# Moving the start of the second layer into the last steps of the first layer's end, and reordering the row sums of the opening stage

## The chip, the cores and the metric

The kernel runs on one core of one Trainium2 chip. The metric is device time in microseconds (us). Before the change three runs took 2792.45, 2796.39 and 2797.21 us; the median is 2796.39. One further execution was recorded by the hardware profiler, and every duration below comes from that record. The engines are called PE (TensorE, matrix products), DVE (VectorE), ACT (ScalarE), POOL (GpSimd) and SP (SyncE, which here only issues transfers). Each engine takes its instructions in the order in which they are queued.

## What is computed

Two graph attention layers on 4096 nodes with 512 features, in fp32. Cut to what matters:

```python
# layer 0
h = relu(layernorm(x))
node_att = softmax(h @ node_w, axis=0)
e = (h @ edge_w) @ (h @ edge_w).T          # 4096 x 4096
e = where(adj > 0, e, -9e15)
x = x + adj * (node_att * softmax(e, axis=1)) @ (h @ weight) + bias
# layer 1, 8 heads of 64
h = relu(layernorm(x))
data1 = (h @ W.T + b).reshape(N, 8, 64)
src, trg = sum(data1 * src_proj, -1), sum(data1 * trg_proj, -1)     # N x 8
e = src.T[:, :, None] + trg.T[:, None, :]
e = where(e >= 0, e, 0.01 * e) + adj                                 # adj as a bias
x = x + concat over heads of softmax(e, axis=-1) @ data1
```

In layer 1 the score is a sum of a source and a target logit but for the leaky step, so its exponential is the larger of two products of a factor of the source node and a factor of the target node. The kernel works with these, with the target logits shifted by their maximum over all nodes (for each head). It calls the target's factors column factors (g, d and what is derived from them) and the source's row factors (z and u).

## The kernel before the change

The 4096 rows are 32 tiles of 128. A block is 512 rows, so there are 8 blocks of 4 tiles. The work goes through five stages, and inside each the instructions stand in an order written by hand.

**Stage 0** (to about 230 us; `fetch`, `stats`, `norm`, `send`, `pull`, `turn`, `row_sums`, `product`, `parts_of`, `step`). Each tile is normalised and transposed, and h is multiplied by `weight` and `edge_w`. From block 1 on, the two products are done by a scheme with seven half-size products per weight instead of eight. It needs four sums of sub-blocks of h for each block (`row_sums`, L251 to L254, on DVE) and sums of the weights (`weight_sums`; its last part, L226, on DVE, overwrites a quarter of the weights once block 0, which uses the plain product, is done). PE's order in block 1 is: products 1 and 2, which need no sums; product 6, which needs the second row sum; product 5, which needs the first row sum and L226; then 7, 3, 4. `step(t)` queues on each engine what tile t and the tiles ahead of it need. `step(6)` turns tiles 6 and 7, and `step(7)` does block 1's row sums before more statistics. `turn` for the first eight tiles ends with `logit` (L158, DVE; L161, POOL), the node attention's logit and the bias sum. The tiles h lie in a ring of four buffers, x in a ring of six.

**Scores of layer 0** (about 230 to 640 us, L538) and **its weighted sums** (to about 1470 us, L751) are not touched by the change.

**The linear stage of layer 1** (`tail`, `linear`, `values`, `logits`, `turn_h`; about 1470 to 1586 us). One step per tile s: DVE adds the bias to the tile before (L894) and turns the next h (L880, a transpose of 32 x 32 squares); PE multiplies tile s by w1 (L887, 8 instructions); POOL multiplies the finished values by the target and the source projection (L898, two products); DVE reduces each per head two steps later (L903), into t_m and s_n. Four PSUM banks hold the results in turn. The output, layernorm and h of layer 0's last block are finished beside the first 20 steps (`ending`). At its end the target maximum is found: a reduction over t_m (L972), a transpose on PE (L978), a reduction, a spread over the partitions by PE (L983) and a copy.

**Layer 1** (L1097 to L1395). For each of 4 blocks of 1024 output nodes and each of 2 sets of 4 heads there is one group of 32 steps, eight groups in all. One step (i, m) takes one tile m of 128 target nodes: `load` (SP, four steps ahead), `exps` (ACT, exp of the adjacency bias into PSUM, L1119), `factors` (ACT, L1129 for head 3 and L1155 for head 0), `weigh` (DVE, up to four products in the order head 3, 0, 1, 2; L1189, and L1186 for head 0; in every fourth step head 0 is done by ACT and POOL), `scale` (POOL for the first steps, then ACT: two heads' values times d), `sums` and the sum of head 3 (POOL), and `gather` (PE, 32 instructions L1223 in two halves and 8 of L1228). `weigh` runs one step ahead of `gather`, `factors` two. Head 3's product reads two SBUF tensors (z and e); the others read z or rl from SBUF and ex from PSUM. Each kind of product has two buffers (head 0: three). At a group's end PE's sums are copied out by ACT: the first quarter in `gather` (L1260), the other three and the denominators one step later in `copy_rest` (L1270, L1272). `tables` prepares the row factors of the later groups in the first steps of group 0.

Between the linear stage and the first step stand the shift by the maximum, the column factors (L1398 to L1406, 128 x 256 elements), the row factors of four heads (L1394, L1395, L1408, L1409) and the first step's four products.

## Time and profile before

| what | value |
|---|---|
| median of three runs | 2796.39 us |
| the profiled execution | 2791.45 us, of it 2789.7 from its first to its last instruction (the span) |
| one step of the linear stage, start to start | 3.43 us |
| end of the last linear product | 1586.03 us after the start |
| end of the second step's products on DVE | 1605.46 us |
| one group of layer 1, from the third on | 146.5 us |

How to read the views. In the list of groups and in the order of time, a row has the start, the duration, the engine, the line of the kernel, the operation and its tiles, then how often; square brackets hold the idle time ahead of it and what ended that. In the list of waits a row has the engine and its line, what it waited for, and the total, the count and the longest in us. In tables by window each engine has its busy time and its count of instructions, followed by the share of full clock that PE was granted, the share of the DMA queues and their rate.

### The profile page before, as it was taken

To read this page: it belongs to the slowest core of one execution; us is meant where nothing else is said; L and a number is where in the kernel's file an instruction comes from. 1 tells how busy PE (TensorE), PEld (TensorE's weight loads), DVE (VectorE), ACT (ScalarE), POOL (GpSimd) and SP (SyncE) were. 2 spreads that over 40 slices of the span, in tenths; PEclk is the share of its full clock that TensorE was granted. 3 is DMA by queue.
4 is the path that set the end of the run, shared out by engine and by line. 5 is a ranking of instruction groups with operands and counts; after the bars stand their busy time and mean duration, and the time that the engine had idled before them with its cause. 6 is when DMAs were issued, how large, how long until landed. Compare 5 with 4: busy or idle time off the path is not lost. (4 is left out here: it accounts for less than half of the span.)

```text
span 2789.7 us, 48939 instructions
## 1 busy us (share of the span) xinstructions
PE 2747.3 (98%) x17835; PEld 1758.8 (63%) x17835; DVE 2504.7 (90%) x3425; ACT 1475.5 (53%) x2218; POOL 1465.5 (53%) x1250
## 2 busy tenths in 40 slices
PE   7999999999999999999999899999999999999999
PEld 4885444445888888888885323464646464655555
DVE  7877789899988888888886799999999999999998
ACT  2212233333133333433332288998888888888786
POOL 5322344444010010111107698888989897979796
PEclk9999999999999999999999899999999999999999
DMA  5636898888999999999967279999999998989897
GB/s 175 177 106 245 292 321 308 303 304 268 206 215 195 201 262 190 234 257 214 236 191 196 81 192 241 241 230 240 222 241 230 242 233 236 229 243 227 217 221 172
DMA packets 536001, 630.00 MB, mean 226 GB/s; under 512 B 292152, under 2 KB 346456, under 8 KB 535760
## 3 DMA queue, kind: packets, MB, share of 16 engines
q1 hardware_dynamic: 461920, 415.87, 49.9%
q0 software_dynamic: 71824, 207.07, 34.4%
q10 hardware_dynamic: 2016, 3.93, 0.4%
q8 instruction: 140, 2.29, 0.3%
q14 instruction: 101, 0.83, 0.1%
HBM read 404.23 MB, written 107.15 MB: 183 GB/s over the span
## 5 line engine op out<-in xcount | busy, mean ns | idle before, releaser
L1223 PE MATMUL pv<-pr,sup 128*32 128x512 f32 x8192 | 1074.1, 594 | 9.7 <-DVE ngd_m L1178 5.5
L1223 PEld LDWEIGHTS pv<-pr,sup 128*32 128x32 f32 x8192 | 503.3, 110 | 411.0 <-issue 163.4
L1189 DVE SCALAR_TENSOR_TENSOR pr<-z,g_m,ex 128x1024 f32<-128x1024 f32 x512 | 630.4, 1270 | 1.5 <-PE dn L1228 0.7
L1200 POOL TENSOR_TENSOR acc<-acc,pr 128x1024 f32<-128x1024 f32 x240 | 576.3, 2401 | 95.0 <-DVE pr L1189 90.5
L1228 PE MATMUL dn<-pr,d_m 128*2 128x512 f32 x1984 | 411.8, 592 | 0.0
L538 PE MATMUL pe<-he_t,he_t 128*128 128x512 f32 x896 | 386.2, 592 | 0.0
L712 ACT ACTIVATE d<-d 128x1024 f32<-128x1024 f32 x126 | 133.1, 1056 | 424.4 <-DVE d L704 222.8
L1189 DVE SCALAR_TENSOR_TENSOR pr<-z,g_m,e 128x1024 f32<-128x1024 f32 x256 | 348.4, 1361 | 0.4 <-ACT e L1129 0.4
L1119 ACT ACTIVATE ex<-e 128x1024 f32<-128x1024 f32 x256 | 263.2, 1028 | 152.7 <-DVE pr L1189 151.7
L538 PEld LDWEIGHTS pe<-he_t,he_t 128*128 128x128 f32 x896 | 169.3, 190 | 210.3 <-issue 194.0
L1129 ACT ACTIVATE e<-e,ld_m 128x1024 f32<-128x1024 f32 x256 | 291.1, 1137 | 0.0
L751 PE MATMUL po<-sup,u 128*128 128x256 f32 x1024 | 263.3, 379 | 0.0
L751 PE MATMUL po<-he_t,at 128*128 128x256 f32 x1024 | 262.9, 379 | 0.0
L1186 DVE SCALAR_TENSOR_TENSOR pr<-rl,ngd_m,ex 128x1024 f32<-128x1024 f32 x191 | 242.7, 1270 | 3.0 <-ACT ex L1119 2.5
L751 PE MATMUL po<-sup,at 128*128 128x256 f32 x1024 | 242.3, 379 | 2.6 <-DVE mc L544 1.5
L840 POOL DMA_DIRECT2D he_t<-he_t x56 | 48.8, 949 | 355.3 <-ACT he_t L754 303.6
L1155 ACT ACTIVATE rl<-z,ngd_m,d_m 128x1024 f32<-128x1024 f32 x191 | 234.9, 1230 | 0.0
L722 DVE TENSOR_TENSOR at<-d,a 128x1024 f32<-128x1024 f32 x126 | 154.2, 1224 | 74.9 <-PE po L751 40.8
L751 PEld LDWEIGHTS po<-sup,at 128*128 128x128 f32 x1024 | 194.2, 190 | 30.0 <-DVE at L722 2.2
L751 PEld LDWEIGHTS po<-he_t,at 128*128 128x128 f32 x1024 | 194.4, 190 | 26.8 <-issue 0.3
L751 PEld LDWEIGHTS po<-sup,u 128*128 128x128 f32 x1024 | 193.9, 190 | 26.1
L543 POOL DMA_DIRECT2D er_d<-mk x136 | 75.0, 551 | 228.9 <-DVE rm L540 216.9
(275 smaller groups left out, 4006.6 us busy)
## 6 DMA issues: line engine op xcount, KB each, us to landing
e<-in_adj_t_dram SPq DMA_DIRECT2D x256, 512.0 KB, 6.2
acc<-pr POOLq DMA_DIRECT2D x192, 512.0 KB, 6.7
a<-in_adj_t_dram SPq DMA_DIRECT2D x126, 512.0 KB, 5.3
ac<-in_adj_t_dram SPq DMA_DIRECT2D x124, 256.0 KB, 4.9
ar<-in_adj_dram SPq DMA_DIRECT2D x120, 256.0 KB, 4.6
ec_d<-mc POOLq DMA_DIRECT2D x120, 256.0 KB, 4.9
er_d<-mk POOLq DMA_DIRECT2D x112, 256.0 KB, 4.5
et<-er_d SPq DMA_DIRECT2D x448, 64.0 KB, 4.1
```

Of the source, the lines that this page charges most:

```text
L538: nc.tensor.matmul(pe[:, :w], he_t[i][:, k, (t % TB) * P:(t % TB + 1) * P], he_t[j][:, k, BL - w:], start=(k == 0), stop=(k == KC - 1))
L712: nc.scalar.activation(d, d, AF.Exp)
L722: nc.vector.tensor_tensor(w, d, aj.pop((n, q)), ALU.mult)
L751: nc.tensor.matmul(acc[:, j, :], A[:, j * P:(j + 1) * P], B, start=(first_ and j == 0), stop=last, skip_group_check=True)
L1119: nc.scalar.activation(x_, ra.pop((i, m)), AF.Exp)
L1129: nc.scalar.activation(x_, ra[i, m], AF.Exp, bias=ld_m[:, h // HG, m:m + 1])
L1155: nc.scalar.activation(r, zs_[i, 0], AF.Relu, bias=ngd_m[:, h // HG, m:m + 1], scale=d_m[:, h, m:m + 1])
L1186: nc.vector.scalar_tensor_tensor(w, rl.pop((i, m)), ngd_m[:, h // HG, m:m + 1], x_, op0=ALU.subtract, op1=ALU.mult)
L1189: p_ = nc.vector.scalar_tensor_tensor(w, zs_[i, k], g_m[:, h + k, m:m + 1], e3.pop((i, m)) if k == 3 else x_, op0=ALU.max, op1=ALU.mult)
L1200: nc.gpsimd.tensor_tensor(acc[i, 3], acc[i, 3], w, ALU.add)
L1223: nc.tensor.matmul(v[c][q][col * Q:(col + 1) * Q, :], va[:, m, g * HG + k, c0:c0 + Q], pr[i, m, k][:, q * BL:(q + 1) * BL], start=(m == 0) ...
L1228: nc.tensor.matmul(dn[col * Q:col * Q + w.shape[1], :], w, src, **fl)
```

## The change

In stage 0, `step(6)` does block 1's row sums and the source weights' last sum right behind the two tiles it turns; the logits of tiles 6 and 7 are held for `step(7)`, with the edge weights' sum. In the linear stage, the weights w1 and the target projection are folded to 512 x 8 weights, and the last eight tiles' target logits are computed from h itself, early, by small products on PE; the maximum, the column factors of the first 24 tiles, the row factors and the first step's products of layer 1 are then made in steps 23 to 31. The last eight columns' factors are made inside layer 1, behind the products of its third step. Two PSUM banks instead of four hold the linear results. Layer 1's buffers lie over those of layer 0. In six steps ACT makes the source reduction instead of DVE. At a group's end two quarters instead of one are copied out at once.

```diff
@@ stage 0
-            logit(t, h)
+            if t < T0 - 2:
+                logit(t, h)
+            else:
+                held.append((t, h))
...
                 if t == T0 - 2:
                     turn(t)
                     turn(t + 1)
-                elif t != T0 - 1:
+                    row_sums(t // TB)
+                    weight_sums("s", ws, last=True)
+                elif t == T0 - 1:
+                    weight_sums("e", we, last=True)
+                    for t_h in held:
+                        logit(*t_h)
+                else:
                     turn(t)
-                if t % TB == TB - 1:
-                    row_sums(t // TB)
+                    if t % TB == TB - 1:
+                        row_sums(t // TB)
...
-        weight_sums("s", ws, last=True)
-        weight_sums("e", we, last=True)
@@ layer 1's buffers (he_t: layer 0's; he_t[2] holds b, the two projections and tab)
+        "pr0": [at_(he_t[3], 1), at_(he_t[2], 0)],
+        "pr2": [at_(he_t[1], 1), at_(he_t[2], 1)],
+        "e3": [flat(ats[0]), at_(he_t[0], 0)],
...
@@ the linear stage
-            vps[t] = bank(PR[t % TB])
+            vps[t] = bank(PR[2 + t % 2])
...
-                eng = nc.vector if t == NT - 1 and key == "t" else nc.gpsimd
-                eng.tensor_tensor(prs[t, key], v, wt[key], ALU.mult)
+                nc.gpsimd.tensor_tensor(prs[t, key], v, wt[key], ALU.mult)
...
+                if key == "s" and t in BY_ACT:
+                    for h in range(H):
+                        nc.scalar.activation(heads(a)[:, h, :], heads(a)[:, h, :], AF.Copy, accum_out=dst[:, h, t:t + 1])
...
+        BY_ACT = range(14, 26, 2)
+        T1 = NT - 2 * TB
+        def prepare(s):
+            if 1 <= s <= KC:
+                nc.gpsimd.tensor_tensor(he_t[4][:, s - 1, :], wt["w1"][:, s - 1, :], wt["t"], ALU.mult)
+            if s == KC + 1:
+                nc.gpsimd.tensor_tensor(he_t[5][:, 0, :], wt["b"], wt["t"], ALU.mult)
+            if KC < s <= 2 * KC:
+                nc.vector.tensor_reduce(wp[:, s - KC - 1, 0:H], heads(he_t[4][:, s - KC - 1, :]), AX.X, ALU.add)
...
+        def early_tiles(s):
+            for k in range(2 * TB):
+                if s == (9 + k if k < TB else 14 + k):
+                    nc.sync.dma_start(he_t[1][:, k % TB, :], h_d[T1 + k])
+                if s == (14 + k if k < TB else 17 + k):
+                    nc.vector.transpose(he_t[3][:, k % TB, :].rearrange("p (k a q) -> p k a q", k=KC, q=S),
...
+        def early_logits(s):
+            for n in range(2):
+                if s == (18, 24)[n]:
...
+                    for k in range(KC):
+                        for g in range(TB):
+                            nc.tensor.matmul(banks["e"][g * S:(g + 1) * S, n * P:(n + 1) * P], wp[:, k, :],
+                                             he_t[3][:, g, k * P:(k + 1) * P], start=(k == 0), stop=(k == KC - 1))
...
+        def column_rest(lo, hi):
+            nc.scalar.activation(d_m[:, :, lo:hi], t_m[:, :, lo:hi], AF.Exp, scale=SLOPE)
+            nc.vector.tensor_scalar(nlg_m[:, :, lo:hi], t_m[:, 0::HG, lo:hi], -(1.0 - SLOPE), None, ALU.mult)
+            nc.vector.scalar_tensor_tensor(ngd_m[:, :, lo:hi], g_m[:, 0::HG, lo:hi], -1.0, d_m[:, 0::HG, lo:hi],
...
+        def layer_1(s):
...
+            if s == 25:
+                nc.vector.tensor_reduce(em, banks["e"][:, 0:2 * P], AX.X, ALU.max)
+                nc.vector.tensor_scalar(x4, gsel, em, None, ALU.mult)
+                nc.vector.tensor_reduce(tm1, t_m[:, :, 0:T1], AX.X, ALU.max)
+                nc.vector.tensor_tensor(tm1, tm1, tb, ALU.subtract)
+                banks["t"] = bank(7)
+                nc.tensor.transpose(banks["t"][:H, 0:P], tm1, ident)
+                nc.tensor.matmul(banks["t"][:H, P:P + TB], sel[:, 0:H], x4, start=True, stop=True)
+                nc.scalar.activation(q_row, ra[0, 0], AF.Exp)
+            if s == 26:
+                nc.vector.tensor_reduce(tmx, banks["t"][:H, 0:P + TB], AX.X, ALU.max)
+                banks["b"] = bank(3)
+                nc.tensor.matmul(banks["b"][:, 0:H], tmx.to_broadcast([H, P]), ident[:H, :H], start=True, stop=True)
+            if s == 27:
+                nc.vector.tensor_tensor(tmb, banks["b"][:, 0:H], tb, ALU.add)
+                column_factors(0, T1)
+                row_factor(3)
+                column_exps(0, T1)
...
+            if s == 28:
+                column_rest(0, T1)
...
+            if s >= 29:
+                first_weigh((3, 0, 1)[s - 29])
+                if s < 31:
+                    first_values(s - 29)
...
-        logits(NT - 2, "t")
-        nc.vector.tensor_reduce(tm1, t_m[:, :, 0:NT - 1], AX.X, ALU.max)
+        logits(NT - 2)
+        first_weigh(2)
         values(NT - 1)
-        logits(NT - 1, "t")
...
@@ layer 1
+                if (i, m, k) == (0, 1, 2):
+                    logits(NT - 1)
...
-                nc.scalar.copy(os_[0][0], v[0][0])
+                for q in range(HV):
+                    nc.scalar.copy(os_[0][q], v[0][q])
...
+                if s == 1 and f is weigh:
+                    column_factors(T1, NT)
+                    column_exps(T1, NT)
+                    column_rest(T1, NT)
```

## The prediction, made before the changed kernel was run

> **What bounds the kernel now.** I read the busy time of the engines first, then the chain that ended last, then TensorE's (PE's) list of waits, then the order of time around each wait.

> ```profile
> PE 2747.3 (98%) x17835; PEld 1758.8 (63%) x17835; DVE 2504.7 (90%) x3425; ACT 1475.5 (53%) x2218; POOL 1465.5 (53%) x1250
> ...
> PE pv L1223 28%; PE dn L1228 8%; DVE pr L1189 3%; PE pt L1299 1%; ACT e L1129 1%; DVE pr L1186 0%; DMA acc<-pr 0%; ACT rl L1155 0%; DVE pr L1367 0%; POOL lg L1144 0%; POOL acc L1200 0%; PE pv L1299 0%; PE pt L1281 0%; ACT ex L1119 0%; ACT z L1395 0%
> ```

> PE is busy 98% of the span, so only its idle time and its slow time can be won, unless another engine sets a stage's pace. The waits are few:

> ```profile
> PE pv L1223 <- DVE ngd_m L1178: 5.5, 1, 5.5
> PE bank L267 <- DVE he_t L252: 3.5, 1, 3.5
> PE pv L1223 <- ACT rl L1155: 3.1, 1, 3.1
> PE po L978 <- DVE tm L976: 2.9, 1, 2.9
> ...
> PE bank L267 <- DVE ws L226: 2.1, 1, 2.1
> ```

> They lie in two places: stage 0 (L267) and the passage to layer 1 (the others). The same two places run on half a clock. Columns below: window, its length, the busy times, then PE's clock, DMA share, GB/s.

> ```profile
> 56.00:62.00 6.00, 3.85 (x9) 2.62 (x9) 5.33 (x11) 1.54 (x3) 1.81 (x2) 0.50 0.75 224
> ...
> 1588.20:1588.50 0.30, 0.00 (x0) 0.00 (x0) 0.00 (x1) 0.00 (x0) 0.30 (x1) 0.65 0.00 0
> 1588.50:1605.00 16.50, 7.10 (x27) 1.93 (x31) 15.10 (x26) 13.10 (x14) 6.87 (x11) 0.50 0.25 78
> ...
> 1600.00:1746.00 146.00, 143.10 (x1262) 46.09 (x1266) 146.00 (x118) 124.05 (x167) 130.47 (x89) 0.98 0.84 213
> ...
> 2045.30:2191.80 146.50, 146.50 (x1477) 82.43 (x1473) 145.87 (x122) 120.55 (x141) 125.57 (x82) 1.00 0.94 236
> ```

> The last two rows matter most: in layer 1's first group VectorE (DVE) is busy 146.00 of 146.00 us and PE is not; from the second group PE is full, with DVE 0.6 us behind. So behind the passage **DVE's start of layer 1 counts, not PE's**.

> **Part 1, stage 0's row sums.** The order of time:

> ```profile
> 51.99 1.74 DVE L251 TENSOR_TENSOR he_t<-h_t 128x512 f32<-128x512 f32 x1
> 53.76 0.69 DVE L252 TENSOR_TENSOR he_t<-he_t,h_t 128x512 f32<-128x512 f32 x1
> 54.60 2.68 PE L267 MATMUL bank<-st,he_t 128*128 128x256 f32 x8 [3.51 <-DVE he_t L252]
> ...
> 58.60 0.68 DVE L226 TENSOR_TENSOR ws<-ws 128x512 f32<-128x512 f32 x1
> 59.43 3.50 PE L267 MATMUL bank<-ws,he_t 128*128 128x256 f32 x8 [2.15 <-DVE ws L226]
> ```

> PE waits 3.51 and 2.15 us, and the two products take 2.68 and 3.50 us against 1.89 at full clock: 0.79 + 1.61 = 2.40. Together 8.1 us, the most this part can give. After the change the copy of tile 6 stays at 45.78, that of tile 7 follows at 46.4 (its transposes ended at 44.2), then four row sums at a pace of 0.61 (47.0 to 49.5), then the weights (50.1). PE wants the second row sum at 51.1 and the weights one product (1.72) later, at 52.8: ready 2.8 and 2.7 us early. All three terms go.

> What is late next is block 2. There DVE's second row sum ends at 78.31 and PE's product that reads it starts at 83.48: 5.2 us of lead. DVE's work up to there is the same (two logits move behind, nothing is added), and only its own short waits for PE vanish (0.32, 0.44, 0.34): 6.3 of 8.1 us. Later blocks follow, since from 105 to 130 us DVE is busy 21.57 of 25. I take **6**. Lower bound 3: the held logits keep two buffers each of rings of four (h) and six (xt), so the norm of tile 10 and the fetch of tile 12 come later; that fetch was issued at 53.24 and its reader waited to 56.50, so 2 to 3 us of lateness would fall on DVE (6.3 - 3.3 = 3). Upper bound 8.1.

> [...]

> **Part 2, the linear stage.** PE gains two groups of 32 instructions (128x32 weights, 128 columns). The nearest row is L1299 of the same form, x32 in 1.09 us, so 2.0 in all; if they didn't overlap in the array, at the 0.15 of a 128x128 transpose (four in 0.60), 9.6. The maximum's matmuls move before the end: PE reaches them in step 25 before DVE's four new small ones (0.41 + 0.17 + 0.36 + 0.16, after 2.46 of usual work from the step's start): 0.4 of waiting, 0.37 and 0.3 of work. **PE: +3.1**, bounds 2 to 11. DVE has 0.96 to spare in each 3.43 us step; eight early transposes (0.70), five reductions of 0.65 and the small ones fit, since six s-reductions (0.67) go to ScalarE (ACT) at eight times 0.30 + 0.19 (rows L1328 and L810), 3.9 of the 6.9 us of two steps. POOL (2.5 of 3.43) takes five more products of 1.25 in steps 1 to 5 and is 2 us late for a while; DVE's transposes stand before the reductions that wait for it, so PE isn't held. SP's eight more loads and earlier ones lie in a stage whose DMA share is low. These I cost at nothing; if the cover fails, POOL's 2 us come through.

> **Part 3, the passage, on DVE.** T is the end of the last linear matmul (1586.03 now). Now DVE ends layer 1's second step (0,1) at 1605.46 = **T + 19.4**. After the change:
> - Steps 27 to 31 add 0.71, 0.38, 1.28, 2.03, 1.27 and drop one transpose (0.70): 4.97 against 4.8 spare. But three of them read two SBUF tensors while POOL works, and such a reader waits: the product of step (0,3) took 2.69 for 1.28 behind POOL's sum. Three waits of 0.9 (up to 1.25, one POOL product) leave DVE 2.8 behind at T (0.1 to 3.9).
> - Then two reductions (1.2, with 0.7 for POOL), the fourth product 1.2, the last bias 0.6: T + 6.5.
> - Step (0,1): head 3, 1.28. Head 0's new buffer lies over the bias and source rows, and POOL reads the latter for tile 31 in two products of 1.25 that start behind head 3: free at T + 10.3. Then 1.27, 1.2, two reductions 1.3, 1.2: **T + 15.2**.
> So 4.2 are won. Behind it the last eight columns' factors stand between steps (0,2) and (0,3): 0.17 on DVE, 0.25 + 0.25 on ACT (64 elements, between rows of 0.23 for 32 and 0.40 for 256), and the exponential of (0,3), 1.13, queued behind them: 1.9, of which 0.7 replaces a wait for POOL that (0,3) has now (1.4). Net **4.2 - 3.1 - 1.2 = about 0**. Bounds: without POOL waits +6; with PE's upper bound and POOL's two products more behind -9.

> [...]

> **Part 4, the seven group borders.** One more output copy is made at once instead of a step later. PE waits for those copies (L1270, 7.8 us over 13 waits, on the weight queue), and the step after a border is 5.12 instead of 4.29. DVE is 0.6 us per group from binding, so at most 0.4 of each 0.8: 0 to 2.8, I take **1**.

> **Sum.** 6 + 0 + 1 = 7 us less. The profiled execution took 2791.45 (span 2789.7, 1.7 around it) and would take 2784.4; the three timed runs lie higher (2792.45 to 2797.21), so against their median 2796.39: **2789.4**. Measuring this kernel can tell about 0.2% (5.6 us) from no change.

> **Rivals.**
> A. Stage 0 alone works, the passage gives its worst half: 6 - 4 + 0 = 2 less, 2794. For it: the POOL waits above. Against: PE idles 11.9 us there now (5.5, 3.1, 2.9, 0.4), and half the clock is gone for 17 us.
> B. The passage works as meant, DVE free of POOL: 8 + 6 + 2 = 16 less, 2780. For it: POOL's first two scalings leave the passage. Against: tile 31's two products enter it.
> C. Slower: **POOL's queue locks DVE.** In steps (0,3), (0,4), (0,6) head 3 now takes 2.69, 2.70, 2.45 for 1.28, 4.0 us in all. If POOL enters step (0,2) more than one sum (2.4 us) behind, each of the eight head-3 products up to (0,9) can wait 1.4: 11.2. With the 1.9 of the late columns and PE's 3.1: 4.2 - 3.1 - 1.9 - 7.2 = -8; stage 0 at its lower 3, the borders 0: 5 slower, 2801. It decides from the point where these waits cost 9 more than now. For it: POOL is busy 130 of 146 us in this group. Against: it drains as soon as ACT takes the scaling at step 6.
> D. The stage 0 order does nothing since the held buffers delay DVE as much: 0 + 0 + 1, 2795.

> **Numbers.** Forecast 45% (its own range 2785 to 2793), A 17%, B 13%, C 15%, D 10%. The range runs from B's 2779 to C's 2802. Faster by over 0.2% holds three quarters of the forecast, B, and a little of A: 0.50. Within: the rest of the forecast, most of A and D: 0.30. Slower: C and something of A and D: 0.20.

> **What would show it.** Right: no L267 wait and full clock between 50 and 65 us; a wait of about 2 us near 75; the linear stage 3 us longer; head-3 products of 2.5 us in layer 1's first steps; DVE's step (0,1) ending some 15 us after T. Wrong: the L267 waits still there; DVE idle in layer 1's first group (then PE or ACT sets it); the 64 new matmuls taking over 4 us; borders still 5.1.

## The result, and the profile after

Six runs of the changed kernel took 2811.30 to 2816.16 us, median **2815.11**; six of the kernel before, on the same chip, took 2792.45 to 2798.52, median 2795.78. The ratio is 1.0069 (95% interval 1.0058 to 1.0079): **0.7% slower**, where 0.25% faster was forecast, and outside the forecast's range (2779 to 2802). The profiled execution has a span of 2813.3 us against 2789.7, so 23.6 us are to be found.

The first part of the page and its chain that ended last (shares of the span) give the first hint.

```profile
PE 2757.5 (98%) x17901; PEld 1773.4 (63%) x17901; DVE 2508.1 (89%) x3436; ACT 1492.6 (53%) x2319; POOL 1471.1 (52%) x1259
...
PE pv L1357 27%; PE dn L1362 8%; PE po L806 6%; PE po L942 3%; DVE he_t L1323 2%; PE pt L1434 1%; PE q L806 1%; DVE at L1323 0%; DVE he_t L1320 0%; ACT he_t L1268 0%; ACT at L1268 0%; SPq L733 0%; DVE pr L1320 0%; DMA a<-in_adj_t_dram 0%; P
```

PE is still busy 98%, but L806, the products of layer 0's weighted sums, now stands in the chain, which before the change reached back only into layer 1. PE's waits, the longest totals first:

```profile
PE q L806 <- DVE d L759: 16.3, 22, 2.0
...
PE bank L270 <- DVE he_t L255: 4.2, 1, 4.2
PE q L806 <- DVE d L766: 3.3, 5, 1.1
...
PE pv L1357 <- DVE he_t L1320: 2.6, 1, 2.6
PE pv L1357 <- DVE he_t L1323: 2.4, 5, 1.5
PE q L806 <- ACT d L767: 1.8, 1, 1.8
```

The three rows of L806 matter here. They name a tile that is new there, q (q2), and they lie in a stage in which PE's list had one row before, from 690 to 1480 us:

```profile
PE po L751 <- DVE at L722: 1.1, 2, 0.7
```

The stages, each from the end of the last one to the end of its own last product (the weighted sums from their first product on), show where the time went. First the kernel before, then the changed one; rows: the weighted sums, the linear stage, layer 1 up to the start of its second group (columns as in the prediction's windows).

```profile
685.06:1473.94 788.88, 787.76 (x3704) 693.88 (x3705) 665.37 (x1004) 272.79 (x419) 77.35 (x91) 1.00 0.92 218
1473.94:1586.03 112.09, 112.09 (x276) 50.34 (x275) 78.73 (x129) 18.17 (x35) 86.22 (x76) 1.00 0.54 147
1586.03:1751.19 165.16, 151.18 (x1317) 48.58 (x1319) 163.00 (x145) 136.49 (x180) 138.77 (x102) 0.95 0.78 201
```

```profile
683.11:1501.63 818.52, 796.98 (x3704) 690.66 (x3705) 666.31 (x1004) 273.95 (x419) 77.33 (x91) 1.00 0.89 210
1501.63:1617.49 115.86, 115.86 (x349) 52.02 (x352) 90.85 (x153) 41.90 (x144) 93.82 (x88) 1.00 0.59 165
1617.49:1775.22 157.73, 149.25 (x1314) 50.69 (x1316) 153.06 (x133) 128.78 (x174) 136.11 (x100) 1.00 0.81 207
```

| part | before, us | after, us | difference | the prediction's sum |
|---|---|---|---|---|
| stage 0, first to last product of the scheme | 177.75 | 175.51 | -2.2 | -6 |
| weighted sums of layer 0 | 788.9 | 818.5 | **+29.6** | not in it |
| linear stage | 112.1 | 115.9 | +3.8 | +3.1 |
| T to the start of layer 1's second group | 165.2 | 157.7 | -7.4 | -3.0 |
| the other seven groups | 1026.3 | 1026.0 | -0.3 | -1 |

In the stage that lost 29.6 us both kernels issue the same number of instructions on every engine (3704, 1004, 419, 91), and DVE's and ACT's busy times agree to 1.2 us. It's not more work; it is waiting. PE's busy time does grow by 9.2 us, but the profile models the ends of the products, which hides a part of each gap. By the starts of the stage's 3584 products (their gaps less the usual 0.216 us), all of the 29.6 us stand at one place, the first of the seven products of a step: 27.2 us ahead of it, in 38 of the 128 steps (before: 1.4, in 2), and 4.2 inside it (before: 0.3), as a product behind a stop runs slower at its start (its four instructions take 1.13 us instead of 1.03).

**The edit behind it** is in the diff, though not in the core shown above, and the text there called the stage untouched. That was wrong:

```diff
+    p_q = l0.enter_context(tc.tile_pool(name="c_q", bufs=1, space=PSUM))
+    q2 = p_q.tile([P, 2, BL], FP, name="q2")
...
         def bank(n):
-            return (p_q if n in (PR[0], "m") else p_o).tile([P, BL], FP, name=f"po{n}")
+            if n in (PR[0], "m"):
+                return q2[:, (PR[0], "m").index(n), :]
+            return (p_r if n in PR[2:4] else p_o).tile([P, BL], FP, name=f"po{n}")
```

Layer 1 wants its exponential in two adjacent PSUM banks, and so one tile of two banks is made early. Until then its halves serve the weighted sums: one is the accumulator of product 1, the first of the seven products of each step, the other the copy of the row maxima ("m"), which DVE subtracts (L759, L766) two steps ahead of the products. Before, these were two tiles. The order of time of the changed kernel, at one step's end:

```profile
703.83 1.03 PE L806 MATMUL po<-he_t,at 128*128 128x256 f32 x4
703.86 1.22 DVE L759 TENSOR_TENSOR d<-d,q 128x1024 f32<-128x1024 f32 x1
...
705.14 1.13 PE L806 MATMUL q<-sup,at 128*128 128x256 f32 x4 [0.28 <-DVE d L759]
```

and of the kernel before at the same place:

```profile
703.84 1.89 PE L751 MATMUL po<-sup,at 128*128 128x256 f32 x8
...
705.60 1.22 DVE L704 TENSOR_TENSOR d<-d,pom 128x1024 f32<-128x1024 f32 x1
```

Before, products 1 and 2 (the row of eight) run on without a gap, and the subtraction comes when DVE gets to it, 1.8 us after product 1's start. After, product 1 (the row that writes q, behind product 4 of the step before) starts only when the subtraction has ended. Product 1 has no use for what L759 makes; the at that it reads was finished before.

**Theory J** (joined tile): an instruction waits for the earlier instructions of the program that use the same tile, whichever half they use; so product 1 (which overwrites nothing of "m") is put behind DVE's reads of "m", and PE, which could run on with what DVE had finished, now stops whenever DVE is late with a later step. **Rival U**: it is the other joined tile of the change, ux, that holds the two sets of sums of at (PE reads one half while DVE writes the other). **Rival D**: neither; the loads of this stage are late (the chain holds pieces of them), or the banks' new places matter.

### The profile page after: what moved, and what is told of

It is laid out like the page before. It is cut to its first block, busy times and chain, and to the rows that moved or that the text cites. A ratio compares the mean times of both kernels' runs of the same rounds, so it can differ in the third digit from the quotient of the medians.

```text
span 2813.3 us, 49148 instructions
## 1 busy us (share of the span) xinstructions
PE 2757.5 (98%) x17901; PEld 1773.4 (63%) x17901; DVE 2508.1 (89%) x3436; ACT 1492.6 (53%) x2319; POOL 1471.1 (52%) x1259
## 3 DMA queue, kind: packets, MB, share of 16 engines
q8 instruction: 140, 2.29, 0.3%
## 4 chain that ended last, share of the span: by engine, by line
PE 47%; DVE 5%; ACT 1%; issue 1%; DMA 1%; POOL 0%; SPq 0%; DVEq 0%; ACTq 0%; POOLq 0%
PE pv L1357 27%; PE dn L1362 8%; PE po L806 6%; PE po L942 3%; DVE he_t L1323 2%; PE pt L1434 1%; PE q L806 1%; DVE at L1323 0%; DVE he_t L1320 0%; ACT he_t L1268 0%; ACT at L1268 0%; SPq L733 0%; DVE pr L1320 0%; DMA a<-in_adj_t_dram 0%; PE po L826 0%
## 5 line engine op out<-in xcount | busy, mean ns | idle before, releaser
L1357 PE MATMUL pv<-he_t,sup 128*32 128x512 f32 x6488 | 994.0, 592 | 7.3 <-DVE he_t L1320 2.6
L1357 PEld LDWEIGHTS pv<-he_t,sup 128*32 128x32 f32 x6488 | 431.3, 110 | 326.3 <-issue 116.0
L1362 PE MATMUL dn<-he_t,acc_z 128*2 128x512 f32 x1984 | 416.2, 592 | 0.0
L767 ACT ACTIVATE d<-d 128x1024 f32<-128x1024 f32 x126 | 133.2, 1057 | 439.7 <-DVE d L759 228.0
L1334 POOL TENSOR_TENSOR acc<-acc,at 128x1024 f32<-128x1024 f32 x120 | 287.7, 2398 | 69.5 <-DVE at L1323 66.2
L1323 DVE SCALAR_TENSOR_TENSOR he_t<-z,rm,q 128x1024 f32<-128x1024 f32 x256 | 315.3, 1271 | 0.4
L1323 DVE SCALAR_TENSOR_TENSOR he_t<-he_t,rm,q 128x1024 f32<-128x1024 f32 x254 | 312.9, 1271 | 1.4 <-ACT q L1258 0.7
L1334 POOL TENSOR_TENSOR acc<-acc,he_t 128x1024 f32<-128x1024 f32 x120 | 287.2, 2393 | 26.4 <-DVE he_t L1323 26.4
L1357 PE MATMUL pv<-at,sup 128*32 128x512 f32 x1024 | 279.9, 593 | 0.2 <-DVE at L1323 0.2
L806 PE MATMUL po<-sup,ux 128*128 128x256 f32 x1024 | 263.3, 379 | 0.0
L806 PE MATMUL po<-he_t,at 128*128 128x256 f32 x1024 | 262.9, 379 | 0.0
L806 PEld LDWEIGHTS po<-he_t,at 128*128 128x128 f32 x1024 | 194.4, 190 | 26.8 <-POOL racc L772 0.3
L806 PEld LDWEIGHTS po<-sup,ux 128*128 128x128 f32 x1024 | 193.9, 190 | 26.1
L1357 PE MATMUL pv<-pr,sup 128*32 128x512 f32 x680 | 187.5, 592 | 0.0
```

The costliest lines, as they stand in the source:

```text
L767: nc.scalar.activation(d, d, AF.Exp)
L806: nc.tensor.matmul(acc[:, j, :], A[:, j * P:(j + 1) * P], B, start=(first_ and j == 0), stop=last, skip_group_check=True)
L1323: p_ = nc.vector.scalar_tensor_tensor(w, zs_[i, k], g_m[:, h + k, m:m + 1], e3.pop((i, m)) if k == 3 else x_, op0=ALU.max, op1=ALU.mult)
L1334: nc.gpsimd.tensor_tensor(acc[i, 3], acc[i, 3], w, ALU.add)
L1357: nc.tensor.matmul(v[c][q][col * Q:(col + 1) * Q, :], va[:, m, g * HG + k, c0:c0 + Q], pr[i, m, k][:, q * BL:(q + 1) * BL], start=(m == 0) ...
L1362: nc.tensor.matmul(dn[col * Q:col * Q + w.shape[1], :], w, src, **fl)
```

## The experiments

**1. The maxima apart from product 1** (e1_m_apart). One edit to the changed kernel; q2 then holds the accumulators of products 1 and 2 (and the early logits of the linear stage go to the bank of the maxima).

```diff
-            if n in (PR[0], "m"):
-                return q2[:, (PR[0], "m").index(n), :]
+            if n in PR[:2]:
+                return q2[:, PR.index(n), :]
```

> The changed kernel, but the big PSUM tile q2 now holds the accumulators of products 1 and 2, and the copy of the maxima ("m") is a tile of its own. Theory J (the joined tile makes product 1 wait for VectorE's reads of the maxima): the weighted sums of layer 0 fall from 818.5 us back to 789 to 793, PE's waits for DVE's d vanish, and the kernel takes 2785 to 2790 us, under the kernel before (2795.8). Rival U (the joined tile of the sums, ux, makes PE and DVE wait for each other): the weighted sums stay at 818, 2815 us in all. Rival D (neither; the loads of this stage or the banks' places): 818 and 2815 too.

Measured: 2794.74 us, ratio to the kernel before 1.0007 (0.9998 to 1.0017); weighted sums 799.4. The waits for DVE's d are gone, 19 of 29.6 us with them. But 10 remained, and the list of waits in this stage says why for most of them:

```profile
PE q L806 <- ACT he_t L809: 7.0, 8, 2.3
```

Eight waits, one for each block: at its end product 2 waits until ACT has copied product 1's sums out, since these two now share the tile. The same mechanism in another place, so J stands; U and D, which expected 818, don't.

**2. The join alone, in the kernel before** (e2_before_joined).

```diff
+        q2 = p_q.tile([P, 2, BL], FP, name="q2")
...
-            return (p_q if n in (PR[0], "m") else p_o).tile([P, BL], FP, name=f"po{n}")
+            if n in (PR[0], "m"):
+                return q2[:, (PR[0], "m").index(n), :]
+            return p_o.tile([P, BL], FP, name=f"po{n}")
```

> The kernel before, with one edit: the accumulator of product 1 and the copy of the maxima become two halves of one PSUM tile. Theory J: the weighted sums go from 788.9 to 815 to 820 us and the kernel from 2795.8 to 2822 to 2827 (it has nothing of the gains of the change). Rivals U and D: 789 and 2796, no change.

Measured: 2823.13 us, ratio 1.0105 (1.0090 to 1.0120); weighted sums 814.5, so +25.6 from this edit alone. The profiled execution was the fastest of the four (2818.48); by the medians (2823.13 against 2793.58) the edit costs 29.5. The stage and its waits:

```profile
685.82:1500.29 814.47, 796.21 (x3704) 691.48 (x3705) 666.15 (x1004) 273.82 (x419) 77.35 (x91) 1.00 0.89 211
```

```profile
PE q L754 <- DVE d L707: 12.9, 19, 1.4
PE q L754 <- DVE d L714: 2.5, 4, 1.1
PE q L754 <- ACT d L715: 1.8, 1, 1.8
```

The same three rows as in the changed kernel (L759, L766, L767 there), in a kernel that has nothing else of the change. J is shown from both sides.

**3. The joined sums alone, in the kernel before** (e3_before_ux).

```diff
-    us_ = [wide.tile([P, 3, BL // 2], FP, name=f"u{n}") for n in range(2)]
+    ux = wide.tile([P, 2, 3, BL // 2], FP, name="ux")
+    us_ = [ux[:, n, :, :] for n in range(2)]
```

> The kernel before, with one edit: the two SBUF tiles of the sums of at become halves of one tile ux. Rival U: the weighted sums go from 788.9 to about 818 us. Theory J and rival D: they stay at 789 (up to 792 if the join costs a little).

Measured: weighted sums 788.8, 2792.42 us in its one run. Rival U falls. A joined tile costs nothing where nobody waits on the other half's user.

**4. Stage 0's new order alone, in the kernel before** (e4_before_stage0). The edit is the diff's first part:

```diff
                     turn(t + 1)
-                elif t != T0 - 1:
+                    row_sums(t // TB)
+                    weight_sums("s", ws, last=True)
...
+                    for t_h in held:
+                        logit(*t_h)
```

> The kernel before with the new order of stage 0 alone (row sums and weights ahead of the last two logits of the first rows). By the prediction's step it gains 6 us: 2790, products of stage 0 ending at 219. By the trace of the changed kernel it gains 2: 2794, products ending at 223.3, with one wait of some 4 us for the second row sum of block 2 and half a clock behind it.

Measured: 2792.52 us, ratio 0.9992 (0.9983 to 1.0002), which alone can't be told from no change; but the products of stage 0 take 175.53 us as in the changed kernel (175.51; 177.75 before). So 2.2 us, not 6, and it is this edit's own doing: the wait for block 2's row sum (L255) is 4.2 us here too, the same that stands ahead of half a clock in the changed kernel (0.50 from 80.24 to 83.65 us).

**5. A better pair for q2** (e5_pair_1_7). As in 1, but products 1 and 7, which stand four and three products apart; the transpose of the maximum in the linear stage then uses product 2's bank.

```diff
+            if n in (PR[0], PR[4]):
+                return q2[:, (PR[0], PR[4]).index(n), :]
```

> The changed kernel with the maxima in a tile of their own, as in the first run, but q2 now holds the accumulators of products 1 and 7, which lie four and three products apart in every step. The trace of the first run showed eight waits of product 2 for the copy of product 1's sums (7.0 us) and a stretch of half clock, 10.5 us of 799.4. If this is all that was left, the weighted sums fall to 789 to 790 and the kernel takes 2783 to 2785 us, ratio to the kernel before 0.9955 to 0.9965. If something else in the change slows this stage, it stays above 795 and the kernel near 2792.

Measured: 2792.52 us, ratio **0.9987** (0.9978 to 0.9996): less than expected. In this profile the weighted sums took 798.2 us, with no wait for a copy and none for d; what was left stood in two places, by the same gaps between starts. Ahead of product 1 there are 5.2 us (before: 1.4), for DVE's tile at, which waits for loads of the adjacency and of the scores; and 6.0 us (before: 0.4) are slow products at half the clock (up to 1.91 us for four instructions that take 1.03 otherwise). In the five later kernels whose stage has the same instructions (runs 6, 8, 9, 10, 12) it took 795.0, 790.1, 797.4, 791.9 and 794.7; where the old tiles are kept (runs 3, 4, 11) 788.8, 790.3 and 792.4. So the stage differs by up to 8 us between executions of the same instructions, through late loads ahead of product 1 and the slow products behind them. The means of the two sets, 794.6 and 790.1 (with the 788.9 of the kernel before), differ by 4.5, less than the spread within one. The medians point the same way: this kernel is 2.9 us faster than the one before, where the gains and losses of its other stages (as in the table) give 6.1, so some 3 us seem still to be lost here. Whether the change makes the loads later is left open, and with it 3 to 5 us.

**6. One logit held in place of two** (e7_hold_one; stage 0, on top of 5).

```diff
-            if t < T0 - 2:
+            if t < T0 - 1:
                 logit(t, h)
```

> The kernel of e5_pair_1_7 with one edit in stage 0: only tile 7's logit is held behind the weights, tile 6's comes at once. Theory H (the two held logits push the norms of tiles 11 and later back, and block 2's second row sum with them): PE has a small wait in block 1 at most (under 1 us), block 2's wait of 4.2 us shrinks to 2 to 3, products of stage 0 end 1 to 3 us earlier than 223. Rival: DVE's work up to block 2 is the same in both, so only the place of the wait moves and stage 0 ends at 223 again.

Measured: 2790.49 us, ratio 0.9981 (0.9972 to 0.9990); stage 0's products take 175.26 us and the wait is 4.0. The rival is right: DVE has the same work up to block 2, so the wait stays where it is.

**7. The join with the step's last product, in the kernel before** (e8_joined_last).

```diff
+            if n in (PR[-1], "m"):
+                return q2[:, (PR[-1], "m").index(n), :]
```

> The kernel before with the copy of the maxima joined into one tile with the accumulator of product 4, the last of a step's seven, in place of product 1, the first. If the price of the join is a wait in the program's order (PE's product behind VectorE's subtraction two steps ahead), it is paid only as far as VectorE is late: product 4 starts some 5 us later in each step, so the weighted sums take 789 to 796 us. If the price came from two engines working on neighbouring banks, the place in the step would not matter and it stays near 814.

Measured: 2802.75 us in its one run; weighted sums 798.9, 10.0 longer than before in place of 25.6. By the gaps 4.6 us stand ahead of product 4, 0.8 more than before ahead of product 1, and 4.7 more are slow products. It is above the expected 796, by the half clock, which wasn't counted. But the price does go with the place in the step: it is a wait in the program's order, paid as far as DVE is late. Run 1 agrees: there product 1's accumulator and the maxima are two tiles, and the 16.3 us of waits for d are gone.

**8. The six source reductions back on DVE** (e9_no_by_act; on top of 5).

```diff
-        BY_ACT = range(14, 26, 2)
+        BY_ACT = ()
```

> The kernel of e5_pair_1_7 with the six source reductions back on VectorE (6 x 0.67 = 4 us more for it in steps 16 to 27 of the linear stage). By the prediction VectorE has 0.96 us to spare in each step of 3.43 but eight transposes and the maximum's reductions in these steps take 6.9: the linear stage grows by 0 to 3 us from 115.8, and layer 1's first steps end up to 3 us later. If it grows by nothing and layer 1 starts as early, moving them was not needed.

Measured: 2787.20 us in its one run, linear stage 115.8, second group at T + 157.7: no difference. The move to ACT wasn't needed; DVE's slack in this stage carries them.

**9. The turned tile's load ahead of the stores of h** (e10_pull_first; stage 0, on top of 8).

```diff
+                upto(pull, t + 2)
                 upto(norm, t + 4)
                 upto(stats, t + 5)
                 upto(send, t + 4)
                 upto(fetch, t + 9 if t >= T0 else t + XT)
-                upto(pull, t + 2)
```

> The kernel of e9_no_by_act with one edit in stage 0: each step issues the load of the turned tile (hq) ahead of the stores of h, behind which it stands on SP's queue. Theory Q (block 2's second row sum is late because the hq load of its last tile waits on that queue behind stores that wait for ScalarE: issued at 73.65, its transpose waited to 77.47): the wait of 4.0 to 4.3 us shrinks to 1 to 3 and the half clock behind it goes; stage 0's products end 1.5 to 4 us earlier, at 219.5 to 222, and the kernel takes 2784 to 2788. Rival: VectorE's own work is what is late (held logits of 2.24 and 2.11, a wait of 1.75 for an x tile): the end stays at 223.

Measured: 2789.07 us, ratio **0.9977** (0.9968 to 0.9986); stage 0's products 173.80 us, the wait 2.8 in place of 4.2. This is the queue it names, SP's in the changed kernel:

```profile
70.33 2.73 SPq L172 DMA_DIRECT2D h_d<-h  x4
73.17 0.38 SPq L136 DMA_DIRECT2D xt<-in_x_dram  x1
73.65 0.55 SPq L178 DMA_DIRECT2D hq<-h_d  x1
```

The last row is the load that DVE's transpose waited for until 77.47. It was ready to go, but stood behind stores of a tile that ACT finished only at 70.3. The half clock didn't go.

**10. GpSimd's first scalings back in layer 1** (e11_values_back; on top of 8).

```diff
-                if s < 31:
-                    first_values(s - 29)
...
+        first_values(0)
+        first_values(1)
         factors(0, 1)
```

> The kernel of e9_no_by_act, but GpSimd's scalings of the values for tiles 0 and 1 go back from steps 29 and 30 of the linear stage to the start of layer 1 (two times two of 0.86 us, behind its two products for tile 31). If the passage gained because GpSimd was free, the first matmuls of layer 1 start 3 to 8 us later, VectorE's products meet GpSimd's sums again, and the second group starts 1 to 6 us later than T + 157.8. If VectorE's moved work alone gave the gain, the second group still starts at T + 157.8.

Measured: 2789.24 us in its one run; the second group starts at T + 158.3 instead of 157.7, layer 1's first product at the same time. So 0.6 of 7.4 us is due to POOL's earlier scalings. The rest, 6.8, is put down to DVE's moved work by the order of time (part 3 below), not by a run of its own.

**11. The border alone, in the kernel before** (e12_border).

```diff
-                nc.scalar.copy(os_[0][0], v[0][0])
+                for q in range(HV):
+                    nc.scalar.copy(os_[0][q], v[0][q])
...
-            for c, q in ((0, 1), (1, 0), (1, 1)):
+            for c, q in ((1, 0), (1, 1)):
```

> The kernel before with the border's edit alone: two output quarters are copied at once instead of one. The prediction's step gives 1 us over seven borders (0 to 2.8); the trace of the changed kernel, where the seven later groups together are 0.3 us shorter, gives 0.3. From T to the last product: 1190.5 by the first, 1191.2 by the second (1191.45 before).

Measured: from T to the last product 1190.6 us against 1191.45: 0.8, near the prediction's 1. A group from the third on takes 146.39 to 146.47 us in place of 146.51 to 146.56 (without the last, 145.89 for 146.03). The one run took 2796.89 us, as other stages were longer in it. In the changed kernel 0.3 of the gain is left: three of its five groups from the third to the seventh still take 146.5.

**12. The x tile's load ahead, too** (e13_fetch_first; from block 2 on, on top of 9).

```diff
                 upto(pull, t + 2)
+                if t >= T0:
+                    upto(fetch, t + 9)
                 upto(norm, t + 4)
                 upto(stats, t + 5)
                 upto(send, t + 4)
-                upto(fetch, t + 9 if t >= T0 else t + XT)
+                if t < T0:
+                    upto(fetch, t + XT)
```

> The kernel of e10_pull_first with one more edit in stage 0: from block 2 on the load of the x tile, too, is issued ahead of the stores of h. There VectorE's wait of 1.77 us for an x tile stands ahead of block 2's second row sum, and PE's wait of 2.8 us and its half clock (3.34 us for a product of 1.89, then two more slow ones) behind it. If the queue's order makes the x tile late, VectorE's wait goes, PE's wait falls to about 1 us and the half clock with it: stage 0's products take 170.5 to 172.5 us instead of 173.8 (177.75 in the kernel before), and the kernel 2784 to 2788. If the tile is late because its buffer comes free late (the copy of the former tile is still being written out), nothing moves: 173.8.

Measured: 2786.78 us, ratio **0.9966** (0.9952 to 0.9980), faster than the kernel before; the interval overlaps that of run 9. The reason given failed: DVE still waits 1.82 us for the x tile (that load is issued in step 7, which the edit leaves as it was), and PE's wait is still 2.8 us. What went is the half clock: 172.46 us for stage 0's products. The last section shows by the windows how one wait of 2.8 us was followed by half the clock and the other wasn't.

## Why the prediction was wrong, step by step

**The step that failed: the weighted sums of layer 0, costed at nothing as "not touched by the change".** The prediction went through what each stage adds and moves, but not through what the new buffers join. q2 stood in the diff, and the row that would have bounded the price was in the trace of before: product 1 starts 1.8 us ahead of the subtraction for a later step, 3.0 ahead of its end (1.8 + 1.22). A join takes that lead, so each of the stage's 128 steps could have lost up to 3.0 us; it lost 0.2 on the mean (25.6 / 128, by run 2), in 38 steps of the changed kernel, since DVE, busy 665 of 789 us, is mostly in time. Even a small share of 128 x 3.0 was more than all that the prediction had in its sum. Runs 1 to 3 show the join as the cause; run 2 puts 25.6 of the 29.6 us on it by its profile, and 29.5 by the medians. Without it (run 5) the kernel is 0.13% faster than before (0.04 to 0.22), where 0.25% was forecast. None of the rivals named this mechanism. Rival C, the one on the slow side, put the loss in layer 1's first steps, where the kernel gained.

**Part 1, stage 0: 6 forecast, 2.2 measured.** All three terms went, as said: no L270 wait in block 1 and full clock there (1.00 from 50 to 65 us), 8.1 us. What comes next was mis-sized. It was written that DVE's second row sum of block 2 comes 1.1 us earlier, as "DVE's work up to there is the same". It ended at 79.63 instead of 78.31, 1.3 later: the held logits took 2.24 and 2.11 us in place of 1.62 each (+1.1), the wait for an x tile grew from 0.57 + 0.26 to 1.75 (+0.9), and a wait of 1.34 for hq, the load of a turned tile, is new; the short waits for PE that vanish give 1.1 back. These terms give 2.2; other rows changed both ways (two more of L158 took 1.34 and 1.67 us and take 0.7 now, and the scheme starts 0.3 later), and 1.3 is left. So PE waits 4.2 and then works at half the clock (3.30 and 2.29 us for products of 1.89: 1.8). 8.1 - 4.2 - 1.8 = 2.1. The lower bound named the held buffers and "2 to 3 us of lateness"; the half clock behind a wait, which had cost 2.40 in block 1 by the prediction's own rows, should have stood in the sum beside it. In size the lower bound, 3, was nearest; rival D named the held buffers, but put the gain at nothing.

**Part 2, the linear stage: +3.1 forecast, +3.8 measured.** The two groups of 32 small products make their steps 1.21 us longer each, so 2.4 (2.0). The maximum's products and their wait take 0.44 + 0.51 = 0.95 (1.07 forecast). The rest, 0.4, is mostly in two steps that are 0.16 and 0.25 longer. What was costed at nothing was nothing: run 8 took even the help for DVE away without loss.

**Part 3, the passage: 3.0 forecast, 7.4 measured.** DVE's order of time in the changed kernel, T = 1617.49:

```profile
1613.96 1.47 DVE L1040 TENSOR_SCALAR he_t<-he_t,rm,acc_z 128x1024 f32<-128x1024 f32 x1
...
1621.95 0.69 DVE L949 TENSOR_TENSOR sup<-po,he_t 128x512 f32<-128x512 f32 x1
1622.56 1.28 DVE L1323 SCALAR_TENSOR_TENSOR at<-he_t,rm,he_t 128x1024 f32<-128x1024 f32 x1
1626.24 1.28 DVE L1320 SCALAR_TENSOR_TENSOR he_t<-ux,mb,q 128x1024 f32<-128x1024 f32 x1 [2.41 <-POOL he_t L955]
...
1629.95 1.28 DVE L1323 SCALAR_TENSOR_TENSOR he_t<-he_t,rm,q 128x1024 f32<-128x1024 f32 x1
...
1637.73 1.28 DVE L1323 SCALAR_TENSOR_TENSOR at<-he_t,rm,he_t 128x1024 f32<-128x1024 f32 x1 [0.86 <-ACT he_t L1268]
```

The path is the one foretold: the last bias, head 3, a wait for POOL's second product of tile 31 (L955), head 0, 1, the reductions, head 2. Step (0,1) ends at 1631.2, T + 13.7, where 15.2 was written and 19.4 was before: 5.7 won instead of 4.2, since DVE is 1.4 us less behind at T than the three assumed waits for POOL made it. The late columns cost 1.2, as written: the lead falls from 5.7 after step (0,2) to 4.5 after (0,3), with the waits of 0.86 and 0.67 for ACT. The term that was missing is a gain: head 3's products in steps (0,4) to (0,6) take 1.28, 1.28 and 1.35 us, where they took 2.70, 1.60 and 2.45 beside POOL's sums; with DVE's start moved they fall between these sums. That gives 2.8 more, 5.7 - 1.2 + 2.8 = 7.3 of the 7.4. Rival C had the same waits with the other sign.

**Part 4, the borders: 1 forecast**, 0.8 alone (run 11), 0.3 within the change. The step after a border does fall from 5.1 to 4.3, but the next one grows from 4.6 to 5.2 or 5.3, so most of the time only moves one step on.

**Against its own signs.** Right: no L270 wait between 50 and 65 us, the linear stage over 3 us longer, step (0,1) near T + 15. Wrong: a wait of 4.2 and not 2 near 75 us, and no head-3 products of 2.5 us. The sum of the parts that it did count would be 2.2 - 3.8 + 7.4 + 0.3 = 6.1 us less, near its 7, by errors that cancel: stage 0 gave 3.8 less, the passage with the linear stage 3.6 more. And the sum was not of the whole kernel.

## What to carry to other kernels

When a change makes one tile of two, or lays a new buffer over old ones early, list every pair of users that it puts on one tile, and for each the lead that the waiting one has now: it is what a step can lose, in a stage whose instructions are all unchanged. If a joined tile can't be avoided, join users that stand far apart in the step. And when a stage's own stall goes, carry the next late thing with its consequences (here the half clock) in the sum, not beside it.

## What the runs showed of the hardware

**In these traces the clock changed in steps of 3.41 us.** The stretches of half clock in these traces last 3.41, 6.8, 10.2, 13.7 or 17.1 us, one to five times 3.41 (but for the one at each trace's end), and start at whole multiples of it after the first rise of the clock: in the kernel before the clock rises at 18.16 us and is halved 37.55 and 1570.13 us later, 11 and 460 times 3.413; in the changed kernel it rises at 18.80 and is halved 61.44 later, 18 times. Runs 9 and 12 have the same wait of 2.8 us in stage 0, and only one pays for it. Run 9, then run 12, by these windows (columns as before; the clock is the third number from the end):

```profile
75.47:78.88 3.41, 1.25 (x6) 0.76 (x4) 3.24 (x7) 0.00 (x0) 2.08 (x2) 1.00 1.04 262
78.88:82.29 3.41, 2.79 (x7) 2.29 (x8) 3.23 (x8) 1.38 (x3) 0.48 (x1) 0.50 0.60 217
```

```profile
74.70:78.11 3.41, 1.69 (x8) 1.14 (x6) 3.16 (x7) 0.36 (x2) 2.32 (x2) 1.00 0.68 177
78.11:81.52 3.41, 2.37 (x11) 2.14 (x12) 3.20 (x9) 0.95 (x2) 0.05 (x1) 1.00 0.91 256
```

In run 9 the wait falls nearly whole into one window, PE is busy 1.25 of 3.41 us there, and the next window has half the clock. In run 12 it is shared out over two, with 1.69 and 2.37 busy, and the clock stays. So the same wait cost 1.3 us more in the one execution (173.80 against 172.46), by its place against the windows.

The busy time of the profile does not draw the border, though. In run 7 a window with the same 1.69 was followed by half the clock:

```profile
1165.87:1169.28 3.41, 1.69 (x8) 0.84 (x6) 3.27 (x4) 1.06 (x1) 0.00 (x0) 1.00 0.76 133
1169.28:1172.69 3.41, 3.41 (x8) 2.78 (x9) 2.13 (x8) 0.81 (x1) 0.00 (x0) 0.50 0.76 181
```

**Scalar products took longer beside POOL.** The prediction's sum had no term for this. In the changed kernel L1040 above took 1.47 us beside POOL's products, where the same form took 0.81 before with POOL idle (L1183), and a 128x48 one (L1021) took 1.01, to 0.04 us behind the end of POOL's product, against 0.19 for its twin L1014 with POOL idle. That is 0.7 and 0.8 us more, 1.5 together.
